# Row numbers by a repeating load for every second range, and the roots of four blocks together

## The chip, the cores and the metric

The kernel runs on one core of one Trainium2 chip. The metric is the device time of one execution in microseconds; a kernel's time is the median of its runs. The profile comes from one further execution under the hardware profiler. The core's engines are TensorE (PE in the profile, PEld for its weight loads), VectorE (DVE), ScalarE (ACT), GpSimd (POOL) and SyncE (SP), which here only issues transfers. Sixteen DMA engines do the transfers of all queues.

## The reference

Two graph layers over 32768 nodes of 128 features and 524288 edges, sorted by destination. Layer 0 sums the source rows of every node's edges, runs a small network on the sum, adds attention inside blocks of 512 nodes and a feed-forward part. Layer 1 repeats three times: a look-up in 512 keys and values, and a normalised sum over the edges. Between the layers stands a layer norm, which is the one that the change touches.

```python
# layer 0
agg = jax.ops.segment_sum(x[src], dst, num_segments=N)
h = (1.0 + eps) * x + agg
...
x = _layernorm(x + _L0_gnn_ref(x, edge_index, ...), axis=-1)
# layer 1, three times (T = 3)
q = x @ Wq.T + bq
attn = jax.nn.softmax(BETA * (q @ keys.T), axis=-1)
retrieved = attn @ values
lap = _laplacian_term(x, row, col)
x = (1.0 - ALPHA) * x + ALPHA * (retrieved - coeff * lap)
```

## The kernel before

Nodes are handled in 64 blocks of 512 (`NB`), each made of four ranges of 128 (`NCH`); there are 256 ranges (`NW`). A sum over edges is done in two passes. The first, the spreading, takes every source range `w` and copies its 128 rows into 1536 slots (`SL`, 12 groups of 128), written to HBM as `slots`; each slot is meant for one destination range. The second pass reads the slots back by destination range and adds them with a 0/1 matrix. There are four such pairs of passes: one in layer 0, three in layer 1. The rows are kept as three bf16 parts side by side, 384 columns (`ROW`), whose sum is the fp32 row.

The spreading of range `w` needs a 0/1 matrix `picks[w]` of 128 x 1536, which says which of the range's 128 rows goes into which slot. It is made from one row of the table `row` (two bytes a number, 1536 numbers a range): `listed_row` (L1418) spreads 512 of these numbers over all partitions by a PE matmul into PSUM (`row_p`, two buffers), and VectorE compares them with the partition's own number `lane1` (L1806). Three such steps `j` make a range's matrix, in fp8. Then `spread` (L1439) does six steps `m`: two PE matmuls of 384 columns into one PSUM tile (`exp`, three buffers of two banks), and one copy of 128 x 768 to the tile `y_o` in SBUF, by ScalarE or by VectorE (`to_dve`). After `m` = 2 and `m` = 5 SP writes half of `y_o` (two buffers) to `slots`.

The first layer's spreading is `spread_x` (L1781). Its order is written out by hand (`manual_schedule`): each engine's queue is the order of the calls. For range `w` it runs the six steps of `spread`; after every odd `m` it makes a third of the next range's matrix; at `m` = 3 it does a quarter of the next block's splitting into bf16 parts (`ends`); after every step `sort_on` adds pieces of a second sort (`build_more`, on VectorE, its operations are L94 and L96) by a quota of time. VectorE copies the tile of `m` = 2, ScalarE the other five. At the first range of a block SP is asked for the `x` rows of the block after next, and the next block's splitting starts.

Layer 1's first stage is in `layer1_grid` (L2133 to L2154). For each block it does three things in a pipeline, set by lists of (place, step) that `placed` merges: `first` (layer 0's last scale, a transpose, the addition of x, the layer norm), `prepare` (split into bf16 parts, the query) and `emit` (look-up with four exponentials, transposes and the 24 spreading steps of its four ranges, every second copy by VectorE). `first` runs for block n+2, `prepare` for n+1, `emit` for n. This stage isn't under `manual_schedule`: the calls give priorities, and the framework settles the order on each engine.

The layer norm (L1072) takes mean and variance on VectorE, the square root on ScalarE (L1083), the reciprocal and the scaling on VectorE. The exponential (L1062) and the square root need different tables in ScalarE, loaded by ACT_TABLE_LOAD.

Of the kernel before, what the change touches and what calls it, by code (L numbers as in the profile page):

```python
# [9 lines left out]
F32 = mybir.dt.float32  # L10
I32 = mybir.dt.int32
BF16 = mybir.dt.bfloat16
FP8 = mybir.dt.float8e4
AF = mybir.ActivationFunctionType
OP = mybir.AluOpType
# [4 lines left out]
P = 128  # L20
D = 128
BLK = 512
NCH = BLK // P
# [885 lines left out]
def tile_gnn_resnorm(ctx: ExitStack, tc: tile.TileContext, a: dict, out: bass.AP):  # L909
# [8 lines left out]
    nc = tc.nc  # L918
    N = a["x"].shape[0]
    E = a["src"].shape[0]  # L920
    NB = N // BLK
    NW = N // P
# [37 lines left out]
    eps_c = cp.tile([P, 1], F32, name="eps_c")  # L960
# [9 lines left out]
    v = {n: vec[:, k:k + 1] for k, n in enumerate(VECS)}  # L970
# [7 lines left out]
    w = {}  # L978
# [117 lines left out]
    def layer_norm(wp, y, o, scale=None, shift=None):  # L1096
        for f in layer_norm_steps(wp, y, o, scale, shift):
            f()
# [222 lines left out]
    SL = 2 * KS * P  # L1321
# [3 lines left out]
    gc = {}  # L1325
# [11 lines left out]
    def rows_of(t, i):  # L1337

        return t.rearrange("(b c p) d -> b p c d", c=NCH, p=P)[i]
# [441 lines left out]
    def spread_x():  # L1781

        ex = Exchange("dst", slots_d[1], rows_d[T_STEPS])
        with tc.tile_pool(name="l0r", bufs=1) as gp, tc.tile_pool(name="l0e", bufs=2) as wp, \
                tc.tile_pool(name="l0e_p", bufs=2, space=PSUM) as p_k, \
                tc.tile_pool(name="l0e_e", bufs=3, space=PSUM) as p_e:
            grid_consts(gp)
            ex.load_rows(gp)
            xb, rows, ends, picks, y = {}, {}, {}, {}, {}
            more = {"steps": grid.build_more(lane, Bank(p_k, "row_p")), "quota": 0.0}  # L1790

            def load(b):
                if b < NB:
                    xb[b] = wp.tile([P, NCH, D], F32, name="xe", bufs=3)
                    nc.sync.dma_start(xb[b], rows_of(a["x"], b))

            def split(b):
                if b < NB:
                    x = xb.pop(b)
                    rows[b], ends[b] = ex.split_steps(wp, b, x, x)  # L1800

            def pick(w, j):
                if w < NW:
                    if j == 0:
                        picks[w] = wp.tile([P, SL], FP8, name="pick", bufs=3)
                    nc.vector.tensor_scalar(picks[w][:, j * BLK:(j + 1) * BLK], ex.listed_row(p_k, "row_p", w, j),  # L1806
                                            gc["lane1"], None, op0=OP.is_equal, saturate=False)

            def sort_on():

                more["quota"] += MORE
                while more["steps"] is not None and more["quota"] > 0:
                    us = next(more["steps"], None)
                    if us is None:
                        more["steps"] = None
                    elif us < 0:
                        more["quota"] = 9 * us * MORE
                    else:
                        more["quota"] -= us

            with tc.manual_schedule():
                load(0)
                load(1)
                split(0)
                for f in ends.pop(0):
                    f()
                for j in range(SL // BLK):
                    pick(0, j)
                for w in range(NW):
                    b, c = divmod(w, NCH)  # L1830
                    if c == 0:
                        load(b + 2)
                        split(b + 1)
                    for m in range(KS):
                        ex.spread(wp, p_e, "exp", w, picks[w], rows[b][:, c, :], m, y, m == 2)
                        if m % 2:
                            pick(w + 1, m // 2)
                        if m == 3 and b + 1 in ends:
                            ends[b + 1][c]()
                        sort_on()  # L1840
                for _ in more["steps"] or ():
                    pass
# [112 lines left out]
    def layer1_grid(v_d, s3, c3):  # L1955

        exs = [Exchange("src", slots_d[t % 2], rows_d[t]) for t in range(T_STEPS)]
        with tc.tile_pool(name="l1g", bufs=1) as gp:
# [6 lines left out]
                if w < NW:  # L1965
                    picked[w] = exs[0].known_pick(wp, w)

            def first(b, st, wp, p_tr):


                def load():
                    st["v"] = wp.tile([P, BLK], F32, name="vT")
                    nc.sync.dma_start(st["v"], v_d[b])
                    st["x0"] = wp.tile([P, NCH, D], F32, name="x1")
                    nc.sync.dma_start(st["x0"], rows_of(a["x"], b))

                def scale():
                    nc.scalar.activation(st["v"], st["v"], AF.Identity, bias=c3, scale=s3)

                def turn():  # L1980
                    st["x"] = wp.tile([P, NCH, D], F32, name="xn", bufs=5)
                    ps = p_tr.tile([P, NCH, P], F32, name="tr")
                    for c in range(NCH):
                        nc.tensor.transpose(ps[:, c, :], st["v"][:, c * P:(c + 1) * P], ident)
                    nc.vector.tensor_add(st["x0"], st["x0"], ps)

                def norm():
                    layer_norm(wp, st["x0"], st["x"])
                    nc.sync.dma_start(kept_of(xs_d[0], b), flat(st["x"]))
                return load, [(7, scale), (12, turn), (15, norm)]  # L1990

            def prepare(t, b, st, wp, p_s, p_tr):

# [139 lines left out]
            with tc.tile_pool(name="l1p", bufs=2) as wp, \  # L2133
                    tc.tile_pool(name="l1p_exp", bufs=2, space=PSUM) as p_e, \
                    tc.tile_pool(name="l1p_s", bufs=2, space=PSUM) as p_s, \
                    tc.tile_pool(name="l1p_tr", bufs=2, space=PSUM) as p_tr:
                sts, firsts = {}, {}
                for w0 in range(2):
                    ask_pick(wp, w0)
                for n in range(-3, NB):  # L2140
                    b = n + 3
                    if b < NB:
                        sts[b] = {}
                        load, firsts[b] = first(b, sts[b], wp, p_tr)
                        load()
                    lists = []
                    if n + 2 in sts:
                        lists.append(firsts.pop(n + 2))
                    if n + 1 in sts:
                        lists.append(prepare(0, n + 1, sts[n + 1], wp, p_s, p_tr))  # L2150
                    if n >= 0:
                        lists.append(emit(0, n, sts[n], wp, p_e, p_s, p_tr, 2))
                    run(placed(*lists))
                    sts.pop(n, None)  # L2154

            with tc.tile_pool(name="l1w", bufs=2) as wp, \
# [4 lines left out]
                for t in range(T_STEPS - 1):  # L2161
                    sums = Sums(exs[t], wp, p_g, gc["iota1"], 2)
                    sts = {}
# [3 lines left out]
                    for n in range(-2, NB):  # L2167
                        lists = []
# [5 lines left out]
                        b = n + 2  # L2174
# [6 lines left out]
            with tc.tile_pool(name="l1z", bufs=2) as wp, \  # L2181
                    tc.tile_pool(name="l1z_r", bufs=1, space=PSUM) as p_r, \
                    tc.tile_pool(name="l1z_seg", bufs=4, space=PSUM) as p_g:
                t = T_STEPS - 1
                ramp = ramp_in_psum(p_r)
                with tc.manual_schedule():
                    ask_part(t, 0, wp)
                    sums = Sums(exs[t], wp, p_g, ramp, 6, 2)
                    ends = []
                    for b in range(NB):  # L2190
                        st = {}
                        run(consume(t, b, st, sums, wp, ends))
                        ends = finish(b, st, wp)
# [82 lines left out]
```

## Time and profile before

| | |
|---|---|
| three runs | 13710.27, 13724.5, 13725.8 us; median 13724.5 |
| profiled execution | 13720.72 us, span 13718.8 us |
| PE busy over the span | 11728.4 us (85%) |
| VectorE busy | 10087.5 us (74%) |
| ScalarE busy | 6762.4 us (49%) |
| mean DMA rate | 262 GB/s |
| spreading of the first layer | from about 3062 to 4293 us of the span |
| layer 1's first stage | from about 6241 to 7650 us |
| table loads in that stage | 126 of 1283 ns |

In the lines of the groups a row reads: line of the code, engine, operation, output and input tiles, their shapes, count; then busy time and mean length of one in ns; then how long the engine idled just before them and what ended that. In the lines of waits: who waited for whom, the total in us, how often, the longest. In the timeline: start, length, engine, line, operation. Instructions that follow each other on one engine overlap a little, so the busy time of an engine is less than the sum of its groups.

### The profile page before, as it was taken

What the parts mean: (1) busy time and instruction counts of PE and PEld (TensorE: products, weight loads), DVE (VectorE), ACT (ScalarE), POOL (GpSimd) and SP (SyncE); (2) the same over time, 40 slices, a digit from 0 to 9 for tenths busy, and PEclk for the clock granted to TensorE, in tenths of its full rate; (3) what the DMA queues carried; (4) which work ended last, traced back from release to release, by engine and by line L of the source; (5) the groups of instructions that cost most, each with busy time, mean ns of one, the idle gap of its engine ahead of it and who ended that gap; (6) DMA issues with size and microseconds to landing.
All of it is one profiled execution on the core that took longest, in us unless ns stands there. A gap on an engine that the chain in (4) does not pass through costs nothing. (4 is left out here: it accounts for less than half of the span.)

```text
span 13718.8 us, 167775 instructions
## 1 busy us (share of the span) xinstructions
PE 11728.4 (85%) x58924; PEld 5767.8 (42%) x58984; DVE 10087.5 (74%) x16572; ACT 6762.4 (49%) x10444; POOL 5314.5 (39%) x5333
## 2 busy tenths in 40 slices
PE   8988898887777888888999799999899999966666
PEld 3333333333333444444444455555455555533333
DVE  6998898879997777767888666666566666566666
ACT  4444444448884111137888566666566666600000
POOL 0000000000003777720000366666566666567777
PEclk9999999999999999999999999999999999988777
DMA  1000000007778999967888899999999999988887
GB/s 41 13 11 12 18 13 11 14 34 277 273 294 312 314 314 315 314 229 261 304 311 310 315 402 401 398 399 399 357 400 400 398 398 401 378 302 289 288 291 256
DMA packets 1339021, 3590.33 MB, mean 262 GB/s; under 512 B 197298, under 2 KB 579154, under 8 KB 1337010
## 3 DMA queue, kind: packets, MB, share of 16 engines
q1 hardware_dynamic: 968816, 2936.78, 56.6%
q0 software_dynamic: 252608, 520.41, 11.9%
q10 hardware_dynamic: 116738, 122.29, 2.6%
q8 instruction: 465, 7.62, 0.2%
q14 instruction: 394, 3.23, 0.1%
HBM read 2075.81 MB, written 1502.97 MB: 261 GB/s over the span
## 5 line engine op out<-in xcount | busy, mean ns | idle before, releaser
L1462 POOL DMA_INDIRECT listed<-rows,other x5120 | 5169.1, 1010 | 4103.9 <-issue 3140.6
L1449 ACT CAST y_o<-exp 128x768 bf16<-128x768 f32 x4352 | 3317.6, 807 | 984.7 <-PE exp L1444 732.6
L1444 PE MATMUL exp<-rows,pick 128*128 128x384 bf16 x12288 | 2818.7, 329 | 414.7 <-ACT y_o L1449 247.9
L1487 PEld LDWEIGHTS <-oh 128*128 128x128 bf16 x19456 | 1982.9, 102 | 2664.4 <-issue 1608.4
L1487 PE MATMUL seg<-y_i,oh 128*128 128x384 bf16 x12288 | 2643.7, 346 | 20.0 <-DMA y_i<-slots 18.7
L1449 DVE CAST y_o<-exp 128x768 bf16<-128x768 f32 x1792 | 1711.3, 955 | 688.9 <-PE exp L1444 576.7
L1444 PEld LDWEIGHTS <-pick 128*128 128x128 fp8e4 x12288 | 1203.3, 98 | 2054.3 <-issue 1371.6
L1487 PE MATMUL seg<-listed,oh 128*128 128x384 bf16 (+1 forms) x5120 | 1303.5, 335 | 885.5 <-DMA listed<-rows,other 848.3
L1390 POOL MEMSET rows<- 128x8 bf16 x64 | 6.8, 107 | 4022.2 <-DMA attn_d<-aT 2859.3
L1639 ACT ACTIVATE pT<-s 128x1024 f32<-128x1024 f32 x1024 | 1027.5, 1025 | 999.5 <-PE s L1614 859.7
L2103 DVE SCALAR_TENSOR_TENSOR part_i<-seg,dinv,part_i 128x128 f32<-128x128 f32 x1536 | 532.6, 347 | 1331.9 <-PE seg L1487 1320.8
L1619 DVE TENSOR_REDUCE mx<-s 128x2 f32<-128x1024 f32 x1024 | 1239.9, 1222 | 312.4 <-PE s L1614 308.4
L1614 PE MATMUL s<-k,q 32*128 32x512 f32 x4096 | 1196.7, 665 | 89.3 <-ACT pT L1639 82.0
L1635 PE MATMUL s<-ql,k 32*128 32x512 f32 x4096 | 1129.4, 646 | 63.8 <-DVE ql L1629 36.1
L1083 ACT ACTIVATE ln_rs<-ln_mv,eps_c 128x4 f32<-128x4 f32 x192 | 57.2, 298 | 1642.2 <-DVE ln_mv L1081 1641.5
L2028 PE MATMUL s<-keysT,qT 128*128 128x512 f32 x1536 | 796.0, 600 | 2.7 <-ACT pr L1062 1.7
L1432 DVE TENSOR_SCALAR_CACHE_REDUCE pick<-row_p,lane 128x512 fp8e4<-128x512 f32 x768 | 555.2, 748 | 260.2 <-PE row_p L1421 243.9
L2040 PE MATMUL s<-pt,values 128*128 128x512 f32 x1536 | 725.9, 595 | 10.7 <-ACT pt L2035 10.4
L1473 DVE TENSOR_TENSOR oh<-iota,slot 128x2432 bf16<-128x2432 bf16 x512 | 724.6, 1415 | 3.0 <-DMA slots<-y_o 3.0
L1473 DVE TENSOR_TENSOR oh<-ramp_p,slot 128x2432 bf16<-128x2432 bf16 x512 | 724.2, 1415 | 3.4 <-DMA slots<-y_o 3.4
L1487 PE MATMUL seg<-common,oh 128*128 128x384 bf16 (+1 forms) x2048 | 632.8, 351 | 69.1 <-DMA common<-rows,shared 68.6
L1421 PE MATMUL row_p<-row,ident_b 128*128 128x512 bf16 x1476 | 587.1, 398 | 95.7 <-DVE pick L1806 88.9
(404 smaller groups left out, 14138.6 us busy)
## 6 DMA issues: line engine op xcount, KB each, us to landing
slots<-y_o SPq DMA_DIRECT2D x2048, 576.0 KB
y_i<-slots SPq DMA_DIRECT2D x1024, 1152.0 KB
pick<-pick SPq DMA_DIRECT2D x1024, 192.0 KB
listed<-rows,other POOLq DMA_INDIRECT x5120
rows<-rows SPq DMA_DIRECT2D x192, 384.0 KB
part_d<-part_o SPq DMA_DIRECT2D x192, 256.0 KB
part_i<-part_d ACTq DMA_DIRECT2D x192, 256.0 KB
rows<-rows SPq DMA_DIRECT2D x64, 386.0 KB
```

The lines of the kernel that those rows point to most:

```text
L1421: nc.tensor.matmul(ps, gc["ident"][:, w % P:w % P + 1].to_broadcast([P, P]), self.row[:, w // P, j * BLK:(j + 1) * BLK], start=True, stop= ...
L1444: nc.tensor.matmul(ps[:, j, :ROW], pick[:, o:o + P], r, start=True, stop=True)
L1449: (nc.vector.tensor_copy if to_dve else nc.scalar.copy)(dst, ps[:, :, :ROW])
L1462: nc.gpsimd.indirect_dma_start(out=g[:, k, :], out_offset=None, in_=self.table, in_offset=bass.IndirectOffsetOnAxis(ap=index[:, k:k + 1], ...
L1473: nc.vector.tensor_tensor(oh.rearrange("p c (w z) -> p c w z", z=2), ramp.rearrange("p (w z) -> p w z", z=2)[:, None].to_broadcast([P, NC2 ...
L1487: nc.tensor.matmul(ps[:, :n], oh[:, j, :], src, start=(k == 0), stop=(k == NC2 - 1))
L1614: nc.tensor.matmul(ps[:, s % 2, :], t["q", o][32 * s:32 * s + 32, c * P:(c + 1) * P], t["k", o][32 * s:32 * s + 32, :], start=True, stop=True)
L1619: nc.vector.tensor_reduce(m[:, c, 2 * i:2 * i + 2, xr[o]], st[b].pop(("two", i)), AX.X, OP.max, negate=True)
L1635: nc.tensor.matmul(ps[:, s % 2, :], t["k", o][32 * s:32 * s + 32, c * P:(c + 1) * P], t["ql", o][32 * s:32 * s + 32, :], start=True, stop= ...
L1639: nc.scalar.activation(t["p", c][:, 2 * i:2 * i + 2, :], ps, AF.Exp)
L2028: nc.tensor.matmul(s, st["q"][:, c * P:(c + 1) * P], keysT, start=True, stop=True)
L2040: nc.tensor.matmul(ps, values[:, k, :], st["pt"][:, k, :], start=(k == 0), stop=(k == NCH - 1))
```

## The change

It has two parts.

In `spread_x`, the matrices of odd ranges are made in another way. `row_of(w)` has SP load the range's row of 1536 numbers from HBM into a new bf16 tile `band` (two buffers), with the same row repeated to all 128 partitions. It is asked for at the start of the odd range before (`w + 2`). One VectorE operation of 1536 elements then compares it with `lane1` and writes the matrix as bf16 (`pick_b`), at `j` = 0; the steps `j` = 1 and 2 do nothing. Even ranges are made as before, with two buffers of the matrix instead of three. For odd ranges VectorE also copies the tile of `m` = 5.

In layer 1's first stage, `first` is split: load, scale, transpose and addition, and the moments run for block n+6, into tiles of a group of four blocks; with the fourth block of a group one square root of all 16 columns of variances and one reciprocal are done; the scaling (`norm`) runs for block n+2. The loop begins four steps earlier, and the tiles that are held longer get more buffers. The arithmetic stays the same.

```diff
--- before.py
+++ after.py
@@ -1786,7 +1786,7 @@
                 tc.tile_pool(name="l0e_e", bufs=3, space=PSUM) as p_e:
             grid_consts(gp)
             ex.load_rows(gp)
-            xb, rows, ends, picks, y = {}, {}, {}, {}, {}
+            xb, rows, ends, picks, bands, y = {}, {}, {}, {}, {}, {}
             more = {"steps": grid.build_more(lane, Bank(p_k, "row_p")), "quota": 0.0}
             def load(b):
@@ -1799,10 +1799,21 @@
                     x = xb.pop(b)
                     rows[b], ends[b] = ex.split_steps(wp, b, x, x)
+            def row_of(w):
+                if w < NW:
+                    bands[w] = wp.tile([P, SL], BF16, name="band")
+                    src = ex.grid["row"][w % P:w % P + 1, w // P * SL:(w // P + 1) * SL]
+                    nc.sync.dma_start(bands[w], src.to_broadcast([P, SL]))
             def pick(w, j):
-                if w < NW:
+                if w < NW and w % 2:
                     if j == 0:
-                        picks[w] = wp.tile([P, SL], FP8, name="pick", bufs=3)
+                        picks[w] = wp.tile([P, SL], BF16, name="pick_b")
+                        nc.vector.tensor_scalar(picks[w], bands.pop(w), gc["lane1"], None, op0=OP.is_equal)
+                elif w < NW:
+                    if j == 0:
+                        picks[w] = wp.tile([P, SL], FP8, name="pick")
                     nc.vector.tensor_scalar(picks[w][:, j * BLK:(j + 1) * BLK], ex.listed_row(p_k, "row_p", w, j),
                                             gc["lane1"], None, op0=OP.is_equal, saturate=False)
@@ -1824,15 +1835,18 @@
                 split(0)
                 for f in ends.pop(0):
                     f()
+                row_of(1)
                 for j in range(SL // BLK):
                     pick(0, j)
                 for w in range(NW):
                     b, c = divmod(w, NCH)
+                    if w % 2:
+                        row_of(w + 2)
                     if c == 0:
                         load(b + 2)
                         split(b + 1)
                     for m in range(KS):
-                        ex.spread(wp, p_e, "exp", w, picks[w], rows[b][:, c, :], m, y, m == 2)
+                        ex.spread(wp, p_e, "exp", w, picks[w], rows[b][:, c, :], m, y, m == 2 or (m == 5 and w % 2))
                         if m % 2:
                             pick(w + 1, m // 2)
                         if m == 3 and b + 1 in ends:
@@ -1965,29 +1979,49 @@
                 if w < NW:
                     picked[w] = exs[0].known_pick(wp, w)
-            def first(b, st, wp, p_tr):
-
+            def first(b, st, wp, p_tr, group):
+                k = b % NCH
                 def load():
-                    st["v"] = wp.tile([P, BLK], F32, name="vT")
+                    st["v"] = wp.tile([P, BLK], F32, name="vT", bufs=3)
                     nc.sync.dma_start(st["v"], v_d[b])
-                    st["x0"] = wp.tile([P, NCH, D], F32, name="x1")
+                    st["x0"] = wp.tile([P, NCH, D], F32, name="x1", bufs=2 * NCH)
                     nc.sync.dma_start(st["x0"], rows_of(a["x"], b))
                 def scale():
                     nc.scalar.activation(st["v"], st["v"], AF.Identity, bias=c3, scale=s3)
                 def turn():
-                    st["x"] = wp.tile([P, NCH, D], F32, name="xn", bufs=5)
                     ps = p_tr.tile([P, NCH, P], F32, name="tr")
                     for c in range(NCH):
                         nc.tensor.transpose(ps[:, c, :], st["v"][:, c * P:(c + 1) * P], ident)
                     nc.vector.tensor_add(st["x0"], st["x0"], ps)
+                def moments():
+                    if k == 0:
+                        group["mv"] = wp.tile([P, NCH, NCH, 2], F32, name="ln_mvs")
+                    st["mv"] = group["mv"]
+                    t = wp.tile([P, NCH, 6], F32, name="ln_st")
+                    for c in range(NCH):
+                        nc.vector.bn_stats(t[:, c, :], st["x0"][:, c, :])
+                        nc.vector.bn_aggr(st["mv"][:, k, c, :], t[:, c, :])
+                    if k == 0:
+                        group["rs"] = wp.tile([P, NCH, NCH], F32, name="ln_rss")
+                    st["rs"] = group["rs"]
+                    if k == NCH - 1:
+                        nc.scalar.activation(st["rs"], st["mv"][:, :, :, 1], AF.Sqrt, bias=eps_c)
+                        nc.vector.reciprocal(st["rs"], st["rs"])
                 def norm():
-                    layer_norm(wp, st["x0"], st["x"])
+                    st["x"] = wp.tile([P, NCH, D], F32, name="xn", bufs=5)
+                    for c in range(NCH):
+                        nc.vector.tensor_scalar(st["x"][:, c, :], st["x0"][:, c, :], st["mv"][:, k, c, 0:1],
+                                                st["rs"][:, k, c:c + 1], op0=OP.subtract, op1=OP.mult)
                     nc.sync.dma_start(kept_of(xs_d[0], b), flat(st["x"]))
-                return load, [(7, scale), (12, turn), (15, norm)]
+                return load, [(7, scale), (12, turn), (15, moments)], [(14, norm)]
             def prepare(t, b, st, wp, p_s, p_tr):
@@ -2134,19 +2168,21 @@
                     tc.tile_pool(name="l1p_exp", bufs=2, space=PSUM) as p_e, \
                     tc.tile_pool(name="l1p_s", bufs=2, space=PSUM) as p_s, \
                     tc.tile_pool(name="l1p_tr", bufs=2, space=PSUM) as p_tr:
-                sts, firsts = {}, {}
+                sts, firsts, norms, group = {}, {}, {}, {}
                 for w0 in range(2):
                     ask_pick(wp, w0)
-                for n in range(-3, NB):
-                    b = n + 3
+                for n in range(-NCH - 3, NB):
+                    b = n + NCH + 3
                     if b < NB:
                         sts[b] = {}
-                        load, firsts[b] = first(b, sts[b], wp, p_tr)
+                        load, firsts[b], norms[b] = first(b, sts[b], wp, p_tr, group)
                         load()
                     lists = []
-                    if n + 2 in sts:
-                        lists.append(firsts.pop(n + 2))
-                    if n + 1 in sts:
+                    if n + NCH + 2 in firsts:
+                        lists.append(firsts.pop(n + NCH + 2))
+                    if n + 2 in norms:
+                        lists.append(norms.pop(n + 2))
+                    if 0 <= n + 1 < NB:
                         lists.append(prepare(0, n + 1, sts[n + 1], wp, p_s, p_tr))
                     if n >= 0:
                         lists.append(emit(0, n, sts[n], wp, p_e, p_s, p_tr, 2))
```

## The prediction

> **What bounds the kernel now.** The chain of waits on the page is cut off after the last block (every share 0%), so it says nothing about the stages of the change. I read the slices instead, to find which engine fills which stage, then the busy times by stretch, then groups and waits inside the two stages that the change touches.
>
> ```profile
> DVE  6998898879997777767888666666566666566666
> ACT  4444444448884111137888566666566666600000
> DMA  1000000007778999967888899999999999988887
> ```
>
> A slice is 343 us. The spreading of the first layer lies in slices 9 to 12 (DVE 9, ACT 8), the first stage of layer 1 in slices 18 to 21 (DVE, ACT 7 to 8, PE 8 to 9). No single engine bounds the whole kernel; what the change gains must be read from these two stages.
>
> ```profile
> core 0: us, PE busy (x) PEld busy (x) DVE busy (x) ACT busy (x) POOL busy (x), PEclk, DMA share, GB/s
> 3062.00:3955.00 893.00, 648.21 (x2899) 297.71 (x2939) 864.85 (x1115) 718.26 (x1022) 4.80 (x45) 0.93 0.72 274
> 3955.00:4293.00 338.00, 251.14 (x1149) 114.67 (x1165) 288.17 (x493) 293.18 (x423) 7.52 (x23) 0.96 0.79 303
> 6270.00:7560.00 1290.00, 1171.74 (x5411) 623.13 (x5409) 1126.39 (x2146) 1149.96 (x1908) 0.00 (x0) 1.00 0.84 307
> ```
>
> Row one is the spreading while the second sort runs beside it (its L94/L96 operations end at about 3955 us): VectorE is busy 864.85 of 893 us, 97%, so it is the bound. Row two is the rest of the spreading: ScalarE 87%, VectorE 85%, DMA 79%; mixed. Row three is layer 1's first stage: PE 91%, ACT 89%, DVE 87%, three engines that hand work to one another.
>
> ```profile
> L1806 DVE TENSOR_SCALAR pick<-row_p,lane 128x512 fp8e4<-128x512 f32 x545 | 399.1, 751 | 24.0 <-PE row_p L1421 21.1 <-PE exp L1444 1.9
> L1449 DVE CAST y_o<-exp 128x768 bf16<-128x768 f32 x181 | 173.0, 956 | 2.1 <-DMA slots<-y_o 2.0
> ```
>
> These are VectorE's groups in row one. The compares are its largest item; 545/3 = 181.7 ranges, so 893/181.7 = 4.92 us a range with 4.76 us of VectorE. All groups there sum to some 952 us over 1115 instructions against 865 busy: neighbours overlap by 0.08 us. So one compare is worth 0.67 us, one eviction 0.88.
>
> ```profile
> PE exp L1444 <- ACT y_o L1449: 49.1, 124, 0.9
> PE exp L1444 <- DVE y_o L1449: 23.3, 48, 0.8
> ...
> PE tr L2034 <- ACT pr L1062: 13.0, 17, 1.3
> PE s L2040 <- ACT pt L2035: 9.5, 26, 0.5
> ...
> PE tr L2034 <- ACT pt L2035: 7.0, 20, 0.3
> ...
> PE s L2011 <- ACT pr L1062: 5.6, 28, 0.3
> ```
>
> PE's waits in row three: on ScalarE 49.1+13.0+9.5+7.0+5.6 = 84 us, on VectorE some 23. PE idles 118 us there, so ScalarE ends most of it.
>
> ```profile
> 6809.24 1.28 ACT L1083 ACT_TABLE_LOAD   x1
> 6810.54 0.30 ACT L1083 ACTIVATE ln_rs<-ln_mv,eps_c 128x4 f32<-128x4 f32 x1
> 6810.74 0.78 ACT L1449 CAST y_o<-exp 128x768 bf16<-128x768 f32 x1
> 6811.42 0.59 ACT L2043 COPY oT<-s 128x512 f32<-128x512 f32 x1
> 6812.02 1.28 ACT L1062 ACT_TABLE_LOAD   x1
> ```
>
> This is ScalarE's timeline in one block: the square root of 128x4 values costs two table loads. After them ScalarE runs almost without a gap until the next retrieval, so they stand where PE waits for it.
>
> **What the Trainium skill says.** "VectorE: DVE Perf Modes", the perf-mode tier table: tensor_scalar on bf16 in SBUF runs four elements a cycle, 693 ns for 2048; any PSUM operand loses that. The trace has no 16-bit tensor_scalar; it has the fp32 form with a per-partition scalar (128x2048, 1286 ns, page 1227), so a pointer scalar doesn't end the fast mode. "ScalarE: Activation LUTs", What ACT_TABLE_LOAD costs: 1283 ns and as much again of drain. The trace agrees with 1283, but shows the next instruction 1.30 us after the load's start, so I use 1.30. "DMA: Bandwidth & Descriptors", Issuing engines are not separate DMA queues: every queue shares 16 engines; the trace gives 274 GB/s at share 0.72, 303 at 0.79, so some 385 GB/s at full share. The same page, Latency and other measured facts, reports copies at half rate when lock-stepped partition streams alias in HBM, by inference; no row here shows it.
>
> **Part 1, the spreading.** For each odd range the change removes three row_p matmuls and three 512-wide compares out of PSUM, and adds one load of 128 times 3 KB (393 KB, 50 MB in all), one 1536-wide 16-bit compare, and moves one eviction (m = 5) from ScalarE to VectorE.
> - The 16-bit compare is not in the trace. Four a cycle at the page's 0.96 GHz: 400 ns plus 140 to 220 fixed (L661: 2304 wide, 1342 ns, is 1200+142; the fp32 row above 1067+219), 0.54 to 0.62; two a cycle 1.0; one a cycle 1.8. I take 0.60, since both dtypes are 16 bits and the operands dense in SBUF; with overlap 0.52.
> - VectorE per pair of ranges: -3 x 0.67 + 0.52 + 0.88 = -0.61, so -0.31 a range: 4.76 to 4.45; at the same 97%, 4.60 instead of 4.92. Over 181.7 ranges that is 57 us. At two a cycle the gain is 20, at one a cycle it is a loss of 55.
> - The work becomes uneven: odd ranges hold three compares and two evictions, even ones nearly nothing. Three PSUM buffers let ScalarE run two evictions ahead, about 1.4 us, and sort steps fill VectorE's light ranges, so I cost this at nothing; without that cover a pair loses up to the difference between ScalarE's five evictions (3.9 us with the splitting's copies) and VectorE's 3.4 us in an even range, 0.5 us, or 45 us in all.
> - The loads stand on SP ahead of the next x load and the next two slot writes. SP issues each in 0.4 us and waits for no new buffer: the two band buffers are read one range before they are asked for again. A band is needed about 1.2 ranges, 5.6 us, after its issue. Bytes rise from 1.35 to 1.54 MB a range; at 4.60 us that is 335 GB/s, share 0.87. Layer 1's first stage runs at 0.84 with only 4.1 us of eviction waits on slot writes, row two at 0.79 with 14.2. I charge 0.05 us a range, 9 us.
> - Row two: 74.3 ranges of 4.55 us. ScalarE loses half an eviction (0.36 us), VectorE 0.31, but the bytes would need a share of 0.94 to use it all. I take 8 us.
> - PE loses 384 matmuls of 0.2 us of streaming, at 73% busy worth nothing; bf16 weights instead of fp8 cost 102 against 98 ns per load in the page's groups, hidden.
> Sum: 57 - 9 + 8 = 56 us.
>
> **Part 2, the roots.** 126 table loads go to at most 32, two for each of 16 groups: 94 x 1.30 = 122 us of ScalarE, 1.9 us a block. Row three holds 59 blocks of 21.9 us, PE 19.9 busy, and 84/59 = 1.4 us of PE waiting on ScalarE. The removed time is larger, but comes in three blocks of four and partly where ScalarE has slack. I take two thirds, 0.95 us, over some 62 blocks: 59 us. From below: a quarter, 22 us, if VectorE (87%) is late next; from above all of it, 87. VectorE's moments and scaling keep their number. Loading four blocks before the first root delays the first spread: VectorE's add and moments are 2.4 us a block, three more of them 7 us, at the other end 3 us come back. Part 2: 55 us. SP's loads of v and x keep their number and only stand earlier.
>
> Sum 111 us. The profiled execution took 13720.7 us (span 13718.8), 4 us under the median of 13724.5; durations are from it, so 13610 there and about 13615 as a median.
>
> **The rivals.**
> - Transfers eat part 1: at share 0.87 and above, slot writes land late, y_o (two buffers) comes free late, and the stage stays as long. For: row two already waits. Against: 0.84 elsewhere does no harm. Only part 2: 13670.
> - ScalarE was not the limit in layer 1: PE and VectorE take up the slack, the longer prologue costs 4. For: VectorE also waits for PE. Against: PE's waits name ScalarE. Only part 1: 13672. Both rivals together: about 13720, no change.
> - Slower: the repeated load. All 128 descriptors read one 3 KB row. A pair of ranges now moves 2.69 MB, 7.0 us at 385 GB/s; the band adds 1.0 us at full rate, and VectorE's 9.2 us is still longer. If the same addresses are served at a third of the rate or less, a band takes over 3.05 us, and 128 x (7.0+3.05) = 1286 us reaches today's 1231 plus part 2's 55: from there the kernel is slower. At 110 GB/s (3.6 us) the stage takes 1357 us, 126 more, and the kernel 13795. For: no load in this trace reads one row so often. Against: halving, the page's case, is not enough.
> - The change doesn't do what it says: the order in layer 1's stage isn't by hand, and the roots could be placed so that tables still alternate; then part 2 falls as in the second rival.
>
> **Numbers.** Forecast, both parts: 44%, its own range 13555 (part 1 without charges and 25 us in row two, 85; part 2 86) to 13665. First rival 16%, second with the fourth 12%, both together 8%, slower 20%. Under about 0.2%, 27 us, a measurement can't tell a change from none. Of the first two rivals 4 points fall within that, of both together 7 and 1 slower. So faster 68%, same 11%, slower 21%. The range, 13555 to 13760, leaves out the slow tail and a little below.
>
> **What would show it.** Right: a 16-bit compare of 0.5 to 0.65 us, 128 times; table loads near 32 in layer 1; the spreading at 4.6 us a range with VectorE over 95%; blocks of layer 1 near 21 us with PE at 95%. Wrong: DMA share of 0.95 or more in the spreading with evictions waiting on slot writes or compares waiting on a band; a compare over 1 us; PE's waits moved from ScalarE to VectorE with the block still at 21.9 us.

## The result, and the profile after

The changed kernel takes 13702.88 us (median of 19 runs), the kernel before 13714.81 (19 runs): ratio 0.999, 95% interval 0.9983 to 0.9997. Some 12 us are gained where 111 were forecast. The profiled execution has a span of 13708.0 us, 10.8 less than before.

The slices of the changed kernel:

```profile
DVE  6998899869987777768888666666566666556666
ACT  4444444447774111137888566666566666600000
...
DMA  1000000019889999967888899999999999988887
```

In slices 9 to 12, the first layer's spreading, ScalarE has gone from 8 to 7 in the first three, VectorE in the third from 9 to 8, and DMA from 7, 7, 7, 8 to 9, 8, 8, 9. In slices 18 to 21 only VectorE's first digit has moved, from 7 to 8; the busy times of the prediction's three stretches, now of the changed kernel, tell more:

```profile
core 0: us, PE busy (x) PEld busy (x) DVE busy (x) ACT busy (x) POOL busy (x), PEclk, DMA share, GB/s
3062.00:3955.00 893.00, 591.46 (x2664) 269.66 (x2707) 828.10 (x1049) 667.67 (x948) 6.76 (x48) 0.94 0.89 319
3955.00:4293.00 338.00, 223.60 (x964) 101.81 (x981) 248.46 (x419) 251.65 (x361) 5.95 (x20) 0.91 0.89 325
6270.00:7560.00 1290.00, 1195.78 (x5547) 637.58 (x5546) 1138.18 (x2127) 1052.82 (x1821) 0.00 (x0) 1.00 0.84 308
```

Row one: VectorE has fallen from 97% to 93%, and the sixteen DMA engines have risen from 0.72 to 0.89. Row two: VectorE and ScalarE are both at 74%, where they were at 85 and 87; now nothing is as full as the transfers. Row three: ScalarE is rid of 97 us, PE has done 24 us more of work in the same time.

The groups of row one that the change moved:

```profile
L1449 ACT CAST y_o<-exp 128x768 bf16<-128x768 f32 x828 | 619.7, 811 | 225.4 <-PE exp L1444 120.2 <-DMA slots<-y_o 92.6 <-DVE y_o L1449 3.0
...
L1449 DVE CAST y_o<-exp 128x768 bf16<-128x768 f32 x276 | 262.2, 950 | 8.0 <-DMA slots<-y_o 4.6 <-PE exp L1444 2.0 <-ACT more_a L111 0.4
...
L1817 DVE TENSOR_SCALAR pick<-row_p,lane 128x512 fp8e4<-128x512 f32 x276 | 205.5, 745 | 30.1 <-PE row_p L1421 25.9 <-PE exp L1444 3.0
```

276 compares are 92 even ranges, so 184 ranges ran in 893 us: 4.85 us a range instead of 4.92. Before ScalarE's evictions (the copies out of PSUM, L1449) stand 92.6 us of waiting for slot writes. In the kernel before it was 7.5 us:

```profile
L1449 ACT CAST y_o<-exp 128x768 bf16<-128x768 f32 x903 | 668.3, 812 | 171.8 <-PE exp L1444 154.4 <-DMA slots<-y_o 7.5 <-ACT y_o L1449 2.8
```

The waits over the whole spreading say who is held up, here in the changed kernel:

```profile
PE exp L1444 <- ACT y_o L1449: 229.6, 448, 3.5
...
ACT y_o L1449 <- DMA slots<-y_o: 129.4, 105, 4.0
PE exp L1444 <- DVE y_o L1449: 95.3, 134, 3.0
...
DVE pick_b L1813 <- DMA band<-row_dst: 43.4, 45, 4.1
```

and in the kernel before:

```profile
PE exp L1444 <- ACT y_o L1449: 103.2, 323, 3.1
...
ACT y_o L1449 <- DMA slots<-y_o: 19.8, 24, 2.8
...
PE exp L1444 <- DVE y_o L1449: 6.2, 17, 0.9
```

One chain read from this is: a slot write lands late, an eviction waits for its half of `y_o`, PE waits for the PSUM tile. A second one is shorter: a band lands late, and VectorE stands still for 43.4 us with its evictions behind. PE's longer waits for evictions are only in part due to these: with all band loads but one left out (e3, below), PE still waits 151.8 us for ScalarE's evictions in row one, against 169.2 in the changed kernel and 67.1 before. From the first to the last eviction the spreading takes 1240.1 us, 1230.5 before. By the evictions' starts the first 176 ranges take 855.8 us instead of 869.3, the other 80 take 384.3 instead of 361.2.

In layer 1's first stage the table loads are 31 instead of 126, 39.7 us instead of 126 x 1.283 = 161.7. Their groups there, in the changed kernel:

```profile
L1062 ACT ACT_TABLE_LOAD x16 | 20.5, 1283 | 0.3
L2015 ACT ACT_TABLE_LOAD x15 | 19.2, 1283 | 0.3
```

What became of them is seen in where two operations of that stage first and last start (the pairs after the colon are shortest, median and longest in ns, then first and last start in us). Before:

```profile
L2043 ACT COPY oT<-s x64: 573/586/588, 6277.8 to 7661.1; 128x512 f32<-128x512 f32 x64
...
L1449 DVE CAST y_o<-exp x768: 928/958/960, 6260.5 to 7708.0; 128x768 bf16<-128x768 f32 x192
```

and after:

```profile
L2077 ACT COPY oT<-s x64: 563/585/592, 6282.2 to 7601.3; 128x512 f32<-128x512 f32 x64
...
L1449 DVE CAST y_o<-exp x768: 926/957/960, 6265.0 to 7693.0; 128x768 bf16<-128x768 f32 x192
```

The first row is the end of a block's look-up, the second is spreading. The last look-up is 60 us earlier, the last eviction only 15. The look-up ran ahead, and 92 us of spreading alone are left behind it, 47 before. In those 92 us PE is half idle:

```profile
7601.00:7693.00 92.00, 49.89 (x243) 23.05 (x241) 63.54 (x73) 51.55 (x68) 0.00 (x0) 1.00 0.84 313
```

PE is busy for 49.89 of the 92 us (in the last 101 us before them, 93.64). The kernel before has the same kind of end, only shorter: 25.51 of its last 47 us.

### The profile page after: what moved, and what is told of

The parts are those of the page before. It is cut to its first block, busy times and chain, and to the rows that moved or that the text cites. A ratio compares the mean times of both kernels' runs of the same rounds, so it can differ in the third digit from the quotient of the medians.

```text
span 13708.0 us, 166668 instructions
## 1 busy us (share of the span) xinstructions
PE 11647.6 (85%) x58536; PEld 5728.5 (42%) x58600; DVE 10012.2 (73%) x16396; ACT 6549.9 (48%) x10174; POOL 5307.9 (39%) x5333
## 5 line engine op out<-in xcount | busy, mean ns | idle before, releaser
L1449 ACT CAST y_o<-exp 128x768 bf16<-128x768 f32 x4224 | 3229.9, 805 | 1166.8 <-PE exp L1444 779.3
L1444 PE MATMUL exp<-rows,pick 128*128 128x384 bf16 x10752 | 2428.0, 328 | 378.7 <-ACT y_o L1449 223.7
L1449 DVE CAST y_o<-exp 128x768 bf16<-128x768 f32 x1920 | 1830.8, 954 | 692.1 <-PE exp L1444 556.1
L1444 PEld LDWEIGHTS <-pick 128*128 128x128 fp8e4 x10752 | 1044.1, 98 | 1728.3 <-issue 1160.5
L1635 PEld LDWEIGHTS s<-ql,k 32*128 32x128 f32 x4096 | 341.7, 190 | 682.3 <-issue 260.6
```

The source lines that it names most:

```text
L1444: nc.tensor.matmul(ps[:, j, :ROW], pick[:, o:o + P], r, start=True, stop=True)
L1449: (nc.vector.tensor_copy if to_dve else nc.scalar.copy)(dst, ps[:, :, :ROW])
L1635: nc.tensor.matmul(ps[:, s % 2, :], t["k", o][32 * s:32 * s + 32, c * P:(c + 1) * P], t["ql", o][32 * s:32 * s + 32, :], start=True, stop= ...
```

## The experiments

Below, "spreading" is the time from the first to the last eviction of the first layer's spreading, "stage" the same for layer 1's first stage. Before: 1230.5 and 1447.8 us; changed: 1240.1 and 1428.0. Each such time comes from one profiled execution. How far they scatter is seen where a stage was left as it is: the old spreading took 1230.0 to 1231.6 us in three kernels, the changed one 1235.8 to 1240.1 in six, the old stage 1447.8 and 1449.1, the changed one 1425.7 to 1433.5 in seven. So a few us of spreading and some 8 us of the stage say nothing. In runs e1 to e8, on two other chips, every kernel took some 14.7 to 14.8 ms, the one before too (e8 alone 15.1), because the later stages, which sum the slots, were slower there; the two stages of the change were not, so these runs are read by stage.

### Each part alone (e1, e2)

e1 takes `spread_x` of the changed kernel and the rest of the one before, e2 the reverse.

> The spreading of the changed kernel with the old first stage of layer 1. Theory: part 1's VectorE time is eaten by late slot writes, so the spreading takes 1232 to 1245 us as in the changed kernel (1240), and the kernel stands within 0.1% of the one before, 13700 to 13725. Rival: part 1 is worth what the prediction said, and only something in the whole changed kernel hid it: spreading at 1175, kernel at about 13660.

> The old spreading with the new first stage of layer 1. Theory: part 2 carries the whole difference: the stage ends 12 to 18 us earlier than before, kernel 0.05 to 0.15% faster, 13695 to 13708. Rival: the two parts disturb each other (DMA state, buffers), and part 2 alone gives the predicted 55: about 13660.

Ratios to the kernel before: e1 1.0003 (0.9991 to 1.0014), e2 0.9998 (0.9986 to 1.0011). By stage: e1 spreading 1235.8, stage 1449.1; e2 spreading 1231.6, stage 1433.5. Neither part gives what was forecast, and neither hides the other: each stage is, within some 5 us, what it is in the changed kernel. On those chips the later stages varied from kernel to kernel by more than e2's 14 us (the last of the four spreadings, which none of them changes, took 2332 to 2391 us in e1 to e4 and 2287 to 2308 in e5 to e8), so its ratio can't show that gain; its stage does.

### The bytes of the band (e3, e4)

```diff
 # e3: one load, used for every odd range
+                    if w > 1:
+                        bands[w] = bands["one"]
+                        return
-                    bands[w] = wp.tile([P, SL], BF16, name="band")
+                    bands[w] = bands["one"] = gp.tile([P, SL], BF16, name="band")
 # e4: every partition loads a row of its own
-                    src = ex.grid["row"][w % P:w % P + 1, w // P * SL:(w // P + 1) * SL]
-                    nc.sync.dma_start(bands[w], src.to_broadcast([P, SL]))
+                    nc.sync.dma_start(bands[w], ex.grid["row"][:, w // P * SL:(w // P + 1) * SL])
```

> The changed kernel, with one band loaded once and used for all odd ranges (every odd range but the first gets the first's slot numbers, so the sums of layer 0 are not the reference's). All instructions of VectorE, ScalarE and PE stay; only 127 of the 128 band loads go. Theory (bytes): evictions no longer wait on slot writes beyond the 20 us of before, the spreading runs at 4.55 to 4.65 us a range beside the sort and takes 1165 to 1190 us instead of 1240. Rival (the work has become uneven between odd and even ranges, three buffers of exp are too few): the spreading stays above 1215.

> The changed kernel, with the band load reading 128 different rows of 3 KB (each partition gets its own row of the table, so the matrices of odd ranges are not the reference's); bytes, descriptors, queue and place stay the same. Theory A (the repetition of one row is what costs): descriptors of 3 KB fall from a mean of 181 ns to 121 to 130, the spreading gains 20 to 45 us. Theory B (the bytes and their place in SP's queue cost, whatever they read): the spreading stays within 8 us of 1240 and evictions wait for slot writes some 100 us as now.

Spreading: e3 1178.2, e4 1204.2. In e3 the share falls to 0.75 and VectorE is back at 95%, as the row of the same stretch says:

```profile
3062.00:3955.00 893.00, 622.32 (x2754) 281.53 (x2798) 845.89 (x1106) 690.03 (x980) 10.76 (x54) 0.93 0.75 289
```

So without the loads the change gives 52 us, of the 65 that the forecast's sum has before its charge for the bytes. In the first 176 ranges it is 40 us (869.3 to 829.8; 57 were forecast for 181.7), in the other 80 it is 13 (361.2 to 348.4; 8 were forecast). The some 15 us missing beside the sort may be the unevenness of the ranges; no run isolates it. The loads take back 58 to 62 (1236 to 1240 against 1178): 22 to 26 in the first 176 ranges, 35 to 36 in the others. What e3 leaves out is the bytes, the load's place in SP's queue and the compare's wait, all at once. e4 gives the gain of theory A: reading own rows brings back 32 to 36 us, 26 stay. Its descriptors did not fall as far as that theory said, to a mean of 147 ns and not of 121 to 130. The DMA records show what was slow. A 3 KB descriptor of the band takes 121 ns in the median in both kernels, but with the one repeated row every tenth takes some 320 ns or more (mean 178), with own rows over 153 (mean 147). With 128 descriptors on 16 engines that is 1.43 and 1.18 us a band, where 0.97 would be all medians.

### A third y_o, with and without the repeated row (e9, e15)

```diff
-                st["y"] = wp.tile([P, 2, KS, ROW], BF16, name="y_o")
+                st["y"] = wp.tile([P, 2, KS, ROW], BF16, name="y_o", bufs=held)   # 3 in spread_x
```

> The changed kernel, with a third y_o tile in the first layer's spreading. The spreading took 1236 to 1240 us with two, 1178 without the band loads' bytes. Theory (the bytes fit, but slot writes land late and hold y_o): with a third tile the evictions' waits on slot writes fall below 30 us and the spreading to 1185 to 1210. Rival (the 16 engines are full at a share of 0.89, a buffer only moves the wait): 1225 or more, share still 0.89.

> The changed kernel with a third y_o tile (1221 us of spreading) and with band loads that read 128 different rows (matrices of odd ranges are not the reference's; 1204 us with two tiles). If the repetition and the two tiles are the two causes of the loss, together they give nearly what leaving out the bands gave: 1175 to 1192. If the bytes alone fill the engines: 1200 or more.

e9: 1220.8, between theory and rival. No eviction's wait on slot writes is left among the forty longest waits of row one, but the share is still 0.89, and two waits stand there: the compare's, whose band comes late, and 39.0 us of ScalarE's evictions for which the profile names no cause ("issue"; 2.5 us before):

```profile
ACT y_o L1449 <- issue: 39.0, 18, 3.0
DVE pick_b L1813 <- DMA band<-row_dst: 31.5, 39, 4.6
```

e15: 1192.4, just over the upper edge of its theory, at a share of 0.90. From 1240, the third tile is worth 19 us and own rows 28 more; the last 14 us to e3's 1178 are left for the bytes, their place in the queue and the late bands together. So only a part of the loss is peculiar to the repeated row, and a high share alone is not what costs most. The 19 us are not all a cost of the loads, either: runs e11 and e12 below load no band after range 184, and there, too, the third tile takes the last 72 ranges from 323.9 us (324.5 in the kernel before) to 314.0. A third tile alone in the kernel before was not run.

### Without the table loads: old and new arrangement (e5, e10)

```diff
 # e5, in the kernel before (shortened: for this stage alone); e10 the same in the group's root
-            nc.scalar.activation(t["rs"], mv[:, :, 1], AF.Sqrt, bias=eps_c)
+            nc.scalar.activation(t["rs"], mv[:, :, 1], AF.Identity, bias=eps_c)
```

> The kernel before, with the square root of the layer norm in layer 1's first stage replaced by a plain copy with bias, which needs no table of its own (the norm divides by the variance and not by its root, so the numbers after it are not the reference's). Everything else stays where it was: no groups of four, no longer prologue. The stage is measured from its first to its last spreading eviction: 1448 us before, 1428 in the changed kernel. Theory (ScalarE's time is not the pace of the spreading; it goes into look-ups that run ahead): the stage falls by at most 25 us, to 1423 or more, though 126 table loads of 1.28 us are gone. Rival (ScalarE is the limit, and the new arrangement in groups of four gives the gain away again): it falls by 50 or more, to 1398 or less.

> The changed kernel, with the square root of a group of four blocks replaced by a plain copy with bias (numbers after the norm are not the reference's), so that no table load is left in layer 1's first stage. Without table loads the old arrangement took 1402 us (1448 with), the new one with 31 loads 1428. Theory (the arrangement itself, with the first steps four blocks ahead, gives the difference away, through the order in which the look-up runs ahead): 1415 to 1432, look-up still 70 us or more ahead at the end. Rival (the remaining loads, and the burst of a group's root, cost the difference): 1405 or less.

Stage: e5 1402.3, e10 1416.0. e5 lies between its theory and its rival, nearer to the rival: 126 table loads less are worth 46 us of the stage. So ScalarE's time did hold up the stage, as the prediction had it, with 46 of the 162 us that the loads took. PE's waits of e5 in a stretch of 1290 us agree, with 25.8 us left for ScalarE's evictions where 49.1 stood:

```profile
PE tr L2035 <- ACT pr L1062: 32.1, 48, 0.7
...
PE exp L1444 <- ACT y_o L1449: 25.8, 38, 3.1
PE s L2041 <- ACT pt L2036: 20.0, 47, 0.5
```

In the arrangement in groups, the same removal leaves more of them, in e10:

```profile
PE exp L1444 <- ACT y_o L1449: 86.8, 148, 1.3
...
PE tr L2068 <- ACT pr L1062: 11.2, 20, 1.3
```

ScalarE is busy only 1014.48 us of the 1290 in e10, less than in e5 (1031.76), so its load is not what makes its evictions late for PE. That it is their places in its queue is what is left, and is argued, not shown; the changed kernel with its 31 loads has 46.2 us in that line and the longer stage. By the stages the arrangement costs 14 us (1402 to 1416), and the 31 loads that stay, with the roots of four blocks in a burst, another 12 (1416 to 1428); both are single runs, not far above the scatter. Theory for e10 also had the look-up 70 us or more ahead at the end. It is 18 us ahead at the last block, in the changed kernel 73, and e10 is only 12 us shorter: so the lead of the look-up can cost at most these 12.

### Another order, other buffers, another split (e6, e7, e8)

All three change the changed kernel's stage: e6 gives `exp` three PSUM tiles and the look-up one each, e7 lets VectorE copy 10 of 24 tiles, e8 fixes the order by the calls.

```diff
 # e6 (s and tr: bufs=1)
-                    tc.tile_pool(name="l1p_exp", bufs=2, space=PSUM) as p_e, \
+                    tc.tile_pool(name="l1p_exp", bufs=3, space=PSUM) as p_e, \
 # e7
-m, y, n % share == share - 1)
+m, y, n % share == share - 1 and not (share == 2 and n % 12 == 11))
 # e8
+                with tc.manual_schedule():
                     for n in range(-NCH - 3, NB):
```

> The changed kernel, with three PSUM tiles for the spreading in layer 1's first stage in place of two; the room comes from the look-up, which gets one tile each for its scores and its transposes in place of two. Theory (the two spreading tiles set the pace): the stage falls from 1428 to 1390 or less. Rival (PE's own work sets it, or the look-up now waits for its single tiles): 1425 or more.

> The changed kernel, with VectorE copying 10 of a block's 24 spreading tiles in that stage instead of 12, ScalarE 14: per block VectorE loses 1.9 us and ScalarE gains 1.6, about what the table loads left free. Theory A (VectorE's slower copy, 0.955 against 0.80 us, holds the two tiles): the stage falls by 10 to 30 us to 1398 to 1418. Theory B (order and PE set the pace): within 8 us of 1428. Theory C (ScalarE still sets it): 1445 or more.

> The changed kernel, with the order of layer 1's first stage fixed by the calls (manual_schedule, as in the first layer's spreading), so that the look-up can't run ahead of the spreading. In the changed kernel the last retrieval stands 92 us before the stage's last eviction, 47 us before. Theory (the freed ScalarE time became lead, which is only cashed in a tail where PE is half idle): with the lead fixed the tail is under 45 us, and the stage falls to 1370 to 1405. Rival (the fixed order makes PE wait for the look-up in every block): the tail is short, but the stage is at 1428 or longer.

Stage: e6 1449.5, e7 1436.6, e8 1794.1. All three are longer than 1428.0: the rivals of e6 and e8, and in e7 a value between B and C. In e8 the tail behind the last look-up is short, 5 us, as both theories had it, but the engines wait for each other in every block:

```profile
DVE y_o L1449 <- PE exp L1444: 222.4, 202, 5.1
ACT oT L2077 <- PE s L2074: 212.8, 46, 6.6
PE exp L1444 <- ACT y_o L1449: 194.1, 271, 2.8
```

The framework's order is far better here than the order of the calls. Each of these edits also changed that order: the last block's retrieval starts 11 us after its first eviction in e7, 73 before it in the changed kernel. So they don't isolate one resource, and say only that these edits found no easy reserve in buffers or split.

### A version with fewer bands, and roots on GpSimd (e11, e12, e13)

```diff
 # spreading, against the changed kernel
+            def by_band(w):
+                return w < 184 and w % 4 == 1
-                        ex.spread(..., m, y, m == 2 or (m == 5 and w % 2))
+                        ex.spread(..., m, y, m == 2)           # e12: and three y_o
 # layer 1, against the kernel before
-            nc.scalar.activation(t["rs"], mv[:, :, 1], AF.Sqrt, bias=eps_c)
+            inverse_root(wp, mv[:, :, 1], t["rs"], nc.gpsimd)  # a seed, three Newton steps
```

> The kernel before with two edits. Spreading: a band only for every fourth range while the sort runs (46 bands, 18 MB in place of 50), no second eviction on VectorE. VectorE per range 4.76 - (3 x 0.67 - 0.52)/4 = 4.39 us, nearly what the change reached (4.45), for a third of the bytes. Layer 1: the inverse square root of each block by 14 small GpSimd operations (Newton steps from a seed out of the exponent), no table load, the old arrangement. Theory: spreading at 1170 to 1195 us, layer 1's stage at 1395 to 1412, kernel 0.5 to 0.7% faster than before. Rival (any band makes slot writes late, and GpSimd's latency or a new order costs the stage its gain): spreading 1215 or more, stage 1425 or more, kernel within 0.2%.

> The kernel of e11 with a third y_o tile in the first layer's spreading. If slot writes still land late there, the spreading is 5 to 25 us shorter than in e11; if VectorE alone sets the pace, within 5 us of it.

> The kernel of e12, with the moments and the GpSimd root one block before the scaling, in place of the same block (the first steps run for block n+3, the scaling for n+2). In e12 VectorE stood 117 us in its queue waiting for GpSimd's last operation, 2.2 us a block, and layer 1's stage took 1546 us. Theory (the wait at the head of VectorE's queue was the whole loss): the wait goes, the stage takes 1400 to 1420 us as without table loads, the spreading 1185 as in e12; kernel 60 to 95 us faster than before. Rival (small GpSimd operations or the moved first steps cost the stage themselves): 1445 or more.

Ratios to the kernel before: e11 1.0044 (1.0027 to 1.006), e12 1.0029 (1.0018 to 1.0039), e13 1.0028 (1.0017 to 1.0039): all three are slower, which neither theory nor rival of e11 had. The spreading, 1206.0 in e11 and 1184.6 in e12, gained: e11 stays 11 us above its theory, and the third tile is worth 21 us more, 10 of them after range 184. The stage lost 80 to 100 us: 1547.3, 1545.6 and, with moments and root called one block earlier than the scaling, 1530.4. The group in e11's 1290 us that points to a reason:

```profile
L1093 DVE TENSOR_SCALAR xn<-x,ln_mv,ln_rs 128x128 f32<-128x128 f32 x216 | 64.8, 343 | 117.3 <-POOL ln_rs L1109 117.3
```

The GpSimd operations take 0.2 us each, 3.9 us one after the other with the steps between them, and the scaling stands at the head of VectorE's queue for 117.3/54 = 2.2 us in each block, with the evictions behind it. e13 was to part the two by a block, and did not: in all 64 blocks the scaling still starts as the chain ends, and its wait is 122.2 us of 1260. Its rival's number came, and it isn't shown that this wait is the whole loss. Why the framework set them next to each other again was not found out; whether a root off ScalarE can reach e5's 1402 stays open.

### What beats both kernels (e14)

e14 has e12's spreading and the changed kernel's layer 1.

> The spreading of e12 (a band for every fourth range beside the sort, three y_o tiles, one eviction in six on VectorE) with the changed kernel's first stage of layer 1 as it is. If the stages add up: spreading 1185, stage 1428, kernel 60 to 70 us faster than before, 0.4 to 0.5%. If layer 0's next stage absorbs the earlier end, as it did with the 5 us of the changed kernel: 15 to 30 us.

13648.13 us (5 runs) against 13712.11 (11 runs) before: ratio 0.9952, interval 0.9938 to 0.9965. Spreading 1186.1, stage 1425.7; the two gains, 44 and 22 us, add up to 66, and the medians differ by 64. At least 11 of the 44 belong to the third tile and to no band: the last 72 ranges, made as in the kernel before, take 313.5 us instead of 324.5.

## Why the prediction was wrong

**The 16-bit compare** was right: 605 to 622 ns for all 128, 614 in the median, where 0.60 was taken. That agrees with the mode of four elements a cycle, 693 ns for 2048, of the Trainium skill ("VectorE: DVE Perf Modes", the perf-mode tier table). VectorE's 828.10 us over 184 ranges are 4.50 us a range, forecast 4.45.

**"I charge 0.05 us a range, 9 us"** is the step of part 1 that failed. The loads cost 58 to 62 us (e3). Two of its terms were too small. A band takes 1.43 us of the sixteen engines and not 1.0; by the shares (0.72 x 4.92 = 3.54, 0.89 x 4.85 = 4.32 us a range) the whole addition is 1.56 a pair of ranges. The "some 385 GB/s at full share" did not hold either: row one now has 319 GB/s at 0.89, which makes 358, and row three of the prediction's own table, 307 at 0.84, already made 365. And the conclusion that a share of 0.87 does no harm came from a stage with other waits: layer 1 evicts into the same two `y_o`, but at 22.3 us for four ranges, 5.6 a range, not 4.6. That a late slot write is hidden there and not here fits this, but no run shows it by itself. The prediction's first rival said this, with these waits, and had 16%. The sign that it gave for itself, a share of 0.95, did not come: the waits did, at 0.89, on slot writes and on bands.

**"I cost this at nothing"**, the unevenness, may have failed too: without the loads VectorE reaches 95% beside the sort and the ranges 4.70 us, where 97% and 4.60 were taken.

**"I take 8 us" for row two** had the wrong sign. From range 176 to the end the spreading took 361 us before and 384 after, while the first 176 ranges gained 14. The relief was there, 13 us without the loads (e3); but the loads cost 35 to 36 in these 80 ranges, more than in the 176 before them. The prediction had noted the 14.2 us of waits on slot writes there, and charged the bytes only with leaving a part of the relief unused.

**The repeated load** was rightly put as a risk, and its price lay far below the point from which it decides: a mean of 178 ns for 121 is two thirds of the full rate, where a third was needed. The half rate that the Trainium skill reports for copies whose rows lie a large power of two apart ("DMA: Bandwidth & Descriptors", Latency and other measured facts) belongs to another pattern, and no run here shows a common cause.

**Part 2: "I take two thirds, 0.95 us, over some 62 blocks: 59 us."** The mechanism was right and the size somewhat high: removing the loads in the old order gives 46 (e5). What failed is the step after it, that the split into groups keeps this but for a longer prologue. The stage's account: 46 for the loads, -14 for the arrangement (e10), -12 for the 31 loads and bursts that stay, so 20 from the first to the last eviction. The prologue was right: from layer 0's last operation to the first eviction it is 43.3 us instead of 38.2, forecast 7 less 3. Together 15, as the stage's end shows (7708.0 to 7693.0). The fourth rival said that the placing isn't by hand and feared alternating tables; the tables did not alternate (31 loads, forecast at most 32). That the places of evictions and look-ups changed is seen in the earlier last look-up; how this costs 14 us stays open. PE reached 92.7% and not 95.

**Both rivals at once**, "no change", had 8%. Its number came, its reasons only by half: the first rival was right, the second (ScalarE not the limit) fell with e5. They were weighed as mishaps of a sum that was likely; but each part added load (bytes, a rearranged queue) to a resource whose reserve had been judged from another stage or not at all. That some 12 us are left in the end is partly luck: the spreading ends 5.8 us later than before, yet layer 0's last operation starts at 6221.7 us, 6222.0 before. Why the stage between took that up is not known; in e14 the spreading ends 36 us earlier, and that came through (6178.8).

**Small slips in the working**, without weight: SP took 0.86 us in the median to issue a band and not 0.4, and the low end of the range counts 85 us where 57 and 25 make 82.

## What to carry to other kernels

Before you trade an engine's time for bytes, divide the transfers' busy time by the shorter stage that you hope for, and count the buffers that a late write or load holds: here 0.72 became 0.89, and two tiles were too few. The share alone doesn't settle it: e15 has 0.90 and is 14 us from e3. Make the trade only where that engine is the bound, and compare at equal buffers: with two tiles a band for every fourth range while the sort ran gave 24 us, for every second one all the way it lost 5 to 10; with three tiles it was 44 and 10. (The sparing version also leaves the last eviction of a range on ScalarE, so the bands are not the only difference.) Where a framework settles the order, price a removal and the rearrangement that it needs apart, by a kernel that leaves the work out in the old order.

## What was not expected of the hardware

- One row of 3 KB read 128 times in a burst: 121 ns a descriptor in the median, as for 128 different rows, but a long tail, a mean of 178 ns against 147, and 321 against 153 at the ninth decile (e4).
- GpSimd took 0.20 to 0.27 us for an operation on 128 x 4 values, and 14 that depend on each other took 3.9 us, longer than the two table loads of 1.28 us that they were to replace.
